# Turning masks over: TensorE transposes against transposing transfers, in a two-layer graph attention kernel

## The chip, the cores and the metric

The kernel runs on one core of a Trainium2 chip. A core has five engines with instruction queues of their own: PE (TensorE: matmuls and transposes, into PSUM), DVE (VectorE), ACT (ScalarE), POOL (GpSimd), and SP (SyncE, which here only issues transfers); 16 DMA engines move the data. The metric is the time of one execution on the device in microseconds (us), from the first instruction to the last.

## The reference

The input is x, 32 graphs (batches) of 512 nodes with 512 features, and for each graph an adjacency matrix of 512x512 integers. Two layers follow one another, each with a layer norm and a relu ahead of it and a residual sum behind it. Cut to what matters, for one graph:

```python
# layer 0: softmax over the row (axis -1), one head
h = maximum(layernorm(x), 0)
s = leaky_relu((h @ w_src)[:, None] + (h @ w_dst)[None, :] + b, 0.2)
x = x + softmax(where(adj + eye == 0, -inf, s), axis=-1) @ h

# layer 1: two GAT layers, softmax over the column (axis 0 of source x destination)
h = maximum(layernorm(x), 0)
mask = (adj > 0) | eye
def gat(h, W, a_src, a_dst):            # for each head
    xl = h @ W
    e = leaky_relu((xl @ a_src)[:, None] + (xl @ a_dst)[None, :], 0.2)
    return softmax(where(mask, e, -1e9), axis=0).T @ xl
h = elu(gat(h, W1, ...) + b1)           # 4 heads of 256, side by side
x = x + gat(h, W2, ...) + b2            # 1 head of 512
```

## The kernel before

Each 512x512 matrix of a batch is held as four row tiles of 128 partitions, `[P, T, N]` with P = 128, T = 4, N = 512. A mask is such a matrix in bf16 that holds 0 where there is an edge and a very large negative number (`NO_EDGE`) where there is none, so that masking is an addition.

**Two orientations of each mask.** The softmax weights E are computed with the source on the partitions, in the layout that the following matmul takes as its stationary operand, and the maximum that the softmax subtracts is taken along the free dimension of the opposite layout. So `edge_weights` (L473) wants a mask twice: `mask_max` for the maximum, `mask` for the weights. Layer 0 gives it `m0` and `m0T`; the five calls of layer 1 (four heads, then the second GAT layer, which the code calls layer 2) give it `m1T` and `m1`. T stands for the transpose.

`edge_weights` runs, for one head:

- `spread` (L462): four PE transposes that put a column of scores into every partition of one PSUM place, `m_row` (one place) or `c_row` (one place);
- `largest` (L480, DVE), four times: the maximum over `mask_max` plus that row;
- two small DVE operations (L486, L488) that make of it the value m to subtract, a second `spread` of m into `m_row` and one of the other scores into `c_row`;
- for each of four tiles: leaky relu on ACT (L498), minus m on DVE (L501), plus `mask` on POOL (L503), exponential on ACT (L506).

Then `aggregate` (L509) multiplies E with the values on PE (L516), into the PSUM places `acc` (four of them).

**How the masks are made.** `masks0` (L566) and `masks1` (L588) load the adjacency of a batch, as bf16, through POOL's queue (L552), turn it into the mask on DVE (L572, L577, L580 for m0; L593, L599 for m1), and call `transposed_mask` (L555). That makes 16 PE transposes of 128x128 bf16 blocks (recorded at L417, in `pe_transpose`) with an identity in bf16 (`ident_b`), four into each of four `acc` places, and four copies out of PSUM by ACT (L450) or DVE (L456), whichever the plan finds free (`evict`, L446).

**Order.** The kernel is written as a list of operations, which `Plan` (L35) orders before anything is emitted. Each operation has an engine (or two to choose from), a cost that is a pair (ns that it keeps its engine or queue, ns until its result is there), and the buffers that it reads and writes. The plan walks through time: on the engine that is free first it starts the ready operation that stands earliest in the list; an operation with `ahead` counts as so many places earlier (`AHEAD` is 400). A buffer gets one of a fixed number of places (`slots`, L243) when an operation on it starts, and gives it back after its last one. `m0`, `m0T`, `m1`, `m1T` and `adj` have one place each, `E` three, `x` two. The SP queue and the issue of transfers are planned as engines too. What comes out is a fixed order of instructions on each engine; at run time each waits on semaphores for what it really needs.

The main loop (L866) works on several batches at once: in pass b it makes the mask of layer 1 and the projection for batch b (`masks1`, `layer1_project`), finishes batch b-1 (`layer2_out`), runs the four heads of batch b, and between them layer 0 of batch b+1 (`layer0_out`, `layer1_in`) and the scores of layer 0 of batch b+2. Batch x goes out to DRAM (`spill`) and comes back in between, on the SP queue, with the loads of x and the stores of the output. The projections (`products`, L665) use seven products of half-size blocks in place of eight, their matmuls are at L717.

Of the kernel before, what the change touches and what calls it, by code (L numbers as in the profile page):

```python
# [9 lines left out]
F32 = mybir.dt.float32  # L10
BF16 = mybir.dt.bfloat16
# [4 lines left out]
P = 128  # L16
# [18 lines left out]
class Plan:  # L35
# [11 lines left out]
    def op(self, engines, cost, emit, reads=(), writes=(), ahead=0, lock=None):  # L47


        i = len(self.ops)  # L50
        after = set()
        for buf, part in reads:
            after.update(buf.wrote.get(part, ()))
        for buf, part in writes:
            after.update(buf.wrote.get(part, ()))
            after.update(buf.read.get(part, ()))
        bufs = []
        for buf, part in (*reads, *writes):
            if buf.kind is not None and buf not in bufs:
                bufs.append(buf)  # L60
                buf.left += 1
                if buf.left == 1 and buf.kind in self.turns:
                    self.turns[buf.kind].append(buf)
        for buf, part in reads:
            buf.read.setdefault(part, []).append(i)
        for buf, part in writes:
            buf.wrote[part] = [i]
            buf.read[part] = []
        after.discard(i)
        self.ops.append((engines if isinstance(engines, tuple) else (engines,), cost, emit, after, bufs, i - ahead, lock))  # L70
# [89 lines left out]
                    known(j)  # L160


def on_pe(n, dtype=F32, transpose=False):
    if transpose:
        return (110.0, 300.0) if dtype == F32 else (68.0, 220.0)
    one = 2 * max(0.8376 * n + 2, 110.0)
    return one, one + 170.0


def on_dve(n, speed=1.0, scaled_psum=False):  # L170
    one = n / 0.96 / speed + (130.0 if scaled_psum else 70.0)
    return one, one + 85.0


def on_act(n, per_partition=0):

    one = n / 1.2 + (80.0, 140.0, 280.0)[per_partition]
    return one, one + 60.0


def on_pool(n, narrow=False):
    one = 2.04 * n + 70.0 if narrow else 2.2 * n + 100.0
    return one, one + 30.0
# [3 lines left out]
def kernel(  # L187
# [24 lines left out]
    nc = tc.nc  # L212
    B, N, D = x.shape
    H, F = att_src1.shape
    HF = H * F
    T = N // P
# [8 lines left out]
    const = ctx.enter_context(tc.tile_pool(name="const", bufs=1))  # L225
# [9 lines left out]
    def node_block(t: int) -> slice:  # L235
        return slice(t * P, (t + 1) * P)


    def places(kind, n, shape, dtype=F32, pool=big):
        return [pool.tile(shape, dtype, tag=f"{kind}{k}", name=f"{kind}{k}") for k in range(n)]  # L240
# [4 lines left out]
        "adj": places("adj", 1, [P, T, N], BF16),  # L245
        "m0": places("m0", 1, [P, T, N], BF16),
        "m0T": places("m0T", 1, [P, T, N], BF16),
        "m1": places("m1", 1, [P, T, N], BF16),
        "m1T": places("m1T", 1, [P, T, N], BF16),
        "h": places("h", 1, [P, T, D + 1]),  # L250
        "hT": places("hT", 1, [P, KD, N]),
# [19 lines left out]
    op = plan.op  # L271


    ident = const.tile([P, P], F32, name="ident")
    make_identity(nc, ident)
    ident_b = const.tile([P, P], BF16, name="ident_b")
    nc.vector.tensor_copy(ident_b, ident)
    off_diag = const.tile([P, P], BF16, name="off_diag")
    nc.vector.tensor_scalar(off_diag, ident, 0.0, None, op0=ALU.is_equal)
    minus_half = const.tile([P, T], F32, name="minus_half")  # L280
# [131 lines left out]
    ROW = range(T)  # L412

    def pe_transpose(ahead, dst, dst_of, src, src_of, identity, part):

        dtype = BF16 if identity is ident_b else F32
        op("PE", on_pe(P, dtype, True), lambda: nc.tensor.transpose(dst_of(), src_of(), identity), src, dst(part), ahead)  # L417

    def layernorm(X):

# [25 lines left out]
    def evict(src, dst, src_of, dst_of, n, bias=None, psum_half=False):  # L446

        def by_act():
            if bias is None:
                nc.scalar.copy(dst_of(), src_of())  # L450
            else:
                nc.scalar.activation(dst_of(), src_of(), AF.Identity, bias=bias)  # L452

        def by_dve():
            if bias is None:
                nc.vector.tensor_copy(dst_of(), src_of())  # L456
            else:
                nc.vector.tensor_scalar(dst_of(), src_of(), -1.0, None, op0=ALU.add)

        op(("ACT", "DVE"), (on_act(n, bias is not None), on_dve(n)), (by_act, by_dve), src, dst)  # L460
# [10 lines left out]
    AHEAD = 400  # L471

    def edge_weights(kind, scores, a_of, c_of, mask_max, mask, junk_of=None):  # L473

        a_row = spread("m_row", scores + mask_max(*ROW), a_of, AHEAD)
        amax, z, m = Buffer("col"), Buffer("col"), Buffer("col")
        for t in range(T):
            def largest(t=t):
                count[0] += 1
                nc.vector.tensor_tensor_reduce(  # L480
                    junk[count[0] % 2], mask_max.at[:, t, :], a_row.at, 1.0, LOWEST, ALU.add, ALU.max,
                    accum_out=amax.at[:, t : t + 1],
                )
            op("DVE", on_dve(N), largest, a_row(*ROW) + mask_max(t), amax(t))
        c_all = lambda: c_of(None)
        op("DVE", on_dve(T), lambda: nc.vector.tensor_add(z.at, c_all(), amax.at), scores + amax(*ROW), z(0))  # L486
        op(
            "DVE", on_dve(T), lambda: nc.vector.scalar_tensor_tensor(m.at, z.at, SLOPE, z.at, op0=ALU.mult, op1=ALU.max),  # L488
            z(0), m(0),
        )  # L490

        E = Buffer(kind)
        m_row = spread("m_row", m(0) + E("place"), lambda t: m.at[:, t : t + 1], AHEAD)
        c_row = spread("c_row", scores + E("place"), c_of, AHEAD)
        for t in range(T):
            op(
                "ACT", on_act(N, 1),
                lambda t=t: nc.scalar.activation(E.at[:, t, :], c_row.at, AF.Prelu, bias=a_of(t), scale=1.0, alpha=SLOPE),  # L498
                c_row(*ROW) + scores, E(t),
            )  # L500
            op("DVE", on_dve(N), lambda t=t: nc.vector.tensor_sub(E.at[:, t, :], E.at[:, t, :], m_row.at), m_row(*ROW) + E(t), E(t))  # L501
            op(
                "POOL", on_pool(N, True), lambda t=t: nc.gpsimd.tensor_add(E.at[:, t, :], E.at[:, t, :], mask.at[:, t, :]),  # L503
                E(t) + mask(t), E(t), lock=True,
            )
            op("ACT", on_act(N), lambda t=t: nc.scalar.activation(E.at[:, t, :], E.at[:, t, :], AF.Exp), E(t), E(t))  # L506
        return E
# [44 lines left out]
        op("POOL", (2200.0, 8000.0), lambda: nc.gpsimd.dma_start(a.at, node_tiles(adj, b)), (), a(0))  # L552
        return a

    def transposed_mask(m, mT, ahead):  # L555
        for k in range(T):
            pt = Buffer("acc")
            view = lambda pt=pt: pt.at[:, : N // 2].bitcast(BF16)
            for t in range(T):
                pe_transpose(  # L560
                    ahead, pt, lambda t=t, view=view: view()[:, node_block(t)], m(t) + mT("place"),
                    lambda t=t, k=k: m.at[:, t, node_block(k)], ident_b, t,
                )
            evict(pt(*ROW), mT(k), view, lambda k=k: mT.at[:, k, :], N)

    def masks0(b):  # L566


        a, m0, m0T, d = load_adj(b), Buffer("m0"), Buffer("m0T"), Buffer("d")
        op(  # L570
            "DVE", on_dve(T * N, 4.0),
            lambda: nc.vector.tensor_scalar(m0.at, a.at, 0.0, NO_EDGE, op0=ALU.is_equal, op1=ALU.mult),  # L572
            a(0), m0(*ROW), lock=True,
        )
        for t in range(T):
            own = node_block(t)
            op("DVE", on_dve(P), lambda t=t, own=own: nc.vector.tensor_add(d.at[:, t, :], a.at[:, t, own], ident), a(0), d(t), lock=True)  # L577
            op(
                "DVE", on_dve(P),
                lambda t=t, own=own: nc.vector.tensor_scalar(  # L580
                    m0.at[:, t, own], d.at[:, t, :], 0.0, NO_EDGE, op0=ALU.is_equal, op1=ALU.mult
                ),
                d(t), m0(t), lock=True,
            )
        transposed_mask(m0, m0T, AHEAD)
        return m0, m0T

    def masks1(b):  # L588

        a, m1, m1T = load_adj(b), Buffer("m1"), Buffer("m1T")  # L590
        op(
            "DVE", on_dve(T * N, 4.0),
            lambda: nc.vector.tensor_scalar(m1.at, a.at, 0.0, NO_EDGE, op0=ALU.is_le, op1=ALU.mult),  # L593
            a(0), m1(*ROW), lock=True,
        )
        for t in range(T):
            own = node_block(t)
            op(
                "DVE", on_dve(P), lambda t=t, own=own: nc.vector.tensor_mul(m1.at[:, t, own], m1.at[:, t, own], off_diag),  # L599
                m1(t), m1(t), lock=True,  # L600
            )
        transposed_mask(m1, m1T, AHEAD)
        M[b] = (m1, m1T)

    slots["d"] = places("d", 1, [P, T, P], BF16)
# [311 lines left out]
```

## Time and profile before

| | |
|---|---|
| time, median of 3 runs | 3947.46 us (3946.25 to 3949.8) |
| span of the profiled run | 3948.1 us |
| two batches (from 1110.81 to 1350.72 us) | 239.91 us |
| PE busy in the first 119 us | 51.0 us |
| transposes of masks on PE (L417, bf16) | 1024, 220 ns each |
| copies of m0T and m1T out of PSUM | 132 on ACT (70.3 us), 124 on DVE (49.6 us) |
| transfers through SP and ACT queues | 138.42 MB + 2.88 MB |
| adjacency through POOL's queue | 33.56 MB |
| x load, spill, load back, output (1 MB each), issue to landing | 5.1, 4.3, 5.7, 4.3 us |
| adjacency load (0.5 MB), issue to landing | 5.8 us |

A row of the groups reads: line, engine, operation, output <- input with the tile names, shape, how many; then busy time and the mean length in ns of one; then how long the engine had been idle just before them and what ended that. In the order of time each row begins with its start and its length in us, and x4 says that four of the same kind in a row are merged. PE records two instructions for each f32 matmul of the program. A list of waits reads: who waited <- for whom: us in total, how many times, the longest. Time that an engine is idle matters only if something else had to wait for it.

### The profile page before, as it was taken

The numbers are of one execution on the slowest core, as the hardware profiler recorded it, in microseconds if no ns is written. First come the engines' busy times: TensorE is split into PE (matmuls) and PEld (weight loads), VectorE is DVE, ScalarE is ACT, GpSimd is POOL, SyncE is SP. The second block draws the span as 40 slices with busy tenths as digits, with TensorE's granted clock in tenths as the row PEclk, the third lists the DMA queues.
The fourth block names the chain that finished last, engine by engine and source line by source line (L and its number), as shares of the span: only waits on it lengthen the run. The fifth ranks groups of instructions, "written<-read, shape, count | busy, mean of one in ns | idle before, by whom it ended". The sixth has DMA issues, their size and how long they took to land.

```text
span 3948.1 us, 54741 instructions
## 1 busy us (share of the span) xinstructions
PE 3860.7 (98%) x20224; PEld 3342.0 (85%) x20224; DVE 2926.7 (74%) x7733; ACT 1715.3 (43%) x2991; POOL 1478.0 (37%) x1306
## 2 busy tenths in 40 slices
PE   4899999999999999999999999999999999999998
PEld 3788888888888888888888888888888888888887
DVE  6887767777777777777777677777777777777764
ACT  2444444444444454444444444444444544444432
POOL 3434333344333343343343433443343433433421
PEclk8999999999999999999999999999999999999999
DMA  4011111111111111111111111111111111111100
GB/s 136 6 54 54 33 49 49 33 54 52 30 49 54 33 54 33 49 49 33 54 54 33 47 50 33 54 44 37 49 48 39 54 33 49 49 33 54 49 22 22
DMA packets 107421, 178.36 MB, mean 45 GB/s; under 512 B 3728, under 2 KB 40592, under 8 KB 107152
## 3 DMA queue, kind: packets, MB, share of 16 engines
q1 hardware_dynamic: 72064, 138.42, 9.5%
q0 software_dynamic: 33792, 33.56, 5.4%
q8 instruction: 158, 2.59, 0.3%
q10 hardware_dynamic: 1296, 2.88, 0.2%
q14 instruction: 111, 0.91, 0.1%
HBM read 141.30 MB, written 67.11 MB: 53 GB/s over the span
## 4 chain that ended last, share of the span: by engine, by line
PE 96%; DVE 2%; DMA 1%; POOL 1%; issue 1%; ACT 0%; SPq 0%; DVEq 0%; ACTq 0%; POOLq 0%
PE acc L516 45%; PE sums L717 22%; PE acc L717 17%; PE acc L417 6%; PE m_row L417 4%; PE c_row L417 2%; DVE junk L307 1%; POOL E_one L503 1%; DMA w<-in_L_gnn_W_dram 0%; DVE E_one L501 0%; ACT E_one L506 0%; DVE junk L480 0%; DMA x<-in_x_dram 0%; DMA w_T<-in_L_gnn_W_dram 0%; DVE w_T L399 0%
## 5 line engine op out<-in xcount | busy, mean ns | idle before, releaser
L516 PE MATMUL acc<-pair,E 128*128 128x257 f32 x4096 | 913.2, 380 | 0.0
L503 POOL TENSOR_TENSOR E<-E,m 128x512 f32<-128x512 f32 x512 | 577.6, 1157 | 825.3 <-DVE E L501 818.3
L516 PEld LDWEIGHTS acc<-pair,E 128*128 128x128 f32 x4096 | 769.2, 189 | 119.2 <-ACT pair L452 5.5
L516 PE MATMUL acc<-h,E_one 128*128 128x256 f32 (+1 forms) x2048 | 501.6, 384 | 6.3 <-ACT E_one L506 3.9
L791 ACT ACTIVATE e<-v,minus_one 128x512 f32<-128x512 f32 x256 | 184.7, 722 | 717.8 <-DVE v L782 682.4
L516 PE MATMUL acc<-xl,E_one 128*128 128x257 f32 (+1 forms) x2048 | 479.5, 381 | 2.7 <-ACT E_one L506 2.7
L480 DVE CUSTOM_DVE_ANT_0 junk<-m1T,m_row 128x512 bf16<-128x512 bf16 x640 | 411.1, 682 | 51.5 <-PE m_row L417 50.9
L506 ACT ACTIVATE E<-E 128x512 f32<-128x512 f32 x512 | 323.6, 632 | 229.6 <-POOL E L503 227.8
L516 PEld LDWEIGHTS acc<-xl,E_one 128*128 128x128 f32 x2048 | 378.6, 190 | 51.8 <-ACT E_one L506 3.1
L516 PEld LDWEIGHTS acc<-h,E_one 128*128 128x128 f32 x2048 | 367.1, 191 | 55.6 <-ACT E_one L506 13.8
L501 DVE TENSOR_TENSOR E<-E,m_row 128x512 f32<-128x512 f32 x512 | 330.3, 679 | 14.7 <-PE m_row L417 12.2
L498 ACT ACTIVATE E<-c_row,pair 128x512 f32<-128x512 f32 x512 | 314.6, 690 | 48.6 <-PE c_row L417 47.7
L717 PE MATMUL acc<-w_T,E 128*128 128x257 f32 (+1 forms) x1024 | 268.1, 384 | 14.7 <-DVE x L534 14.7
L794 DVE SCALAR_TENSOR_TENSOR v<-e,v 128x512 f32<-128x512 f32 x256 | 177.7, 694 | 138.8 <-ACT e L791 134.6
L534 DVE SCALAR_TENSOR_TENSOR x<-acc,r,x 128x256 f32<-128x256 f32 x512 | 244.8, 479 | 46.3 <-PE acc L516 43.7
L717 PE MATMUL sums<-w_T,E 128*128 128x257 f32 (+1 forms) x1024 | 271.6, 381 | 0.0
L717 PE MATMUL acc<-w,E 128*128 128x257 f32 (+1 forms) x1024 | 264.6, 381 | 0.0
L503 POOL TENSOR_TENSOR E_one<-E_one,m0T 128x512 f32<-128x512 f32 x128 | 146.5, 1176 | 309.8 <-DVE E_one L501 309.8
L506 ACT ACTIVATE E_one<-E_one 128x512 f32<-128x512 f32 x256 | 161.3, 630 | 232.1 <-POOL E_one L503 228.9
L782 DVE SCALAR_TENSOR_TENSOR v<-acc,r,b_r 128x256 f32<-128x256 f32 x512 | 246.2, 481 | 13.7 <-DVE r L779 0.4
L779 DVE RECIPROCAL r<-acc 128x1 f32<-128x1 f32 x512 | 83.5, 163 | 214.1 <-PE acc L516 211.5
L503 POOL TENSOR_TENSOR E_one<-E_one,m 128x512 f32<-128x512 f32 x128 | 144.3, 1160 | 234.1 <-DVE E_one L501 234.1
(123 smaller groups left out, 6750.1 us busy)
## 6 DMA issues: line engine op xcount, KB each, us to landing
x<-in_x_dram SPq DMA_DIRECT2D x32, 1024.0 KB, 5.1
adj<-in_adj_dram POOLq DMA_DIRECT2D x64, 512.0 KB, 5.8
spill<-x SPq DMA_DIRECT2D x32, 1024.0 KB, 4.3
x<-spill SPq DMA_DIRECT2D x32, 1024.0 KB, 5.7
out_dram<-x SPq DMA_DIRECT2D x32, 1024.0 KB, 4.3
w<-in_L_gnn_W_dram SPq DMA_DIRECT2D x6, 256.0 KB, 9.0
w<-in_L_gnn_W_dram SPq DMA_DIRECT2D x8, 127.5 KB, 4.9
w_T<-in_L_gnn_W_dram SPq DMA_DIRECT2D x4, 128.5 KB, 5.8
```

The costliest lines, as they stand in the source:

```text
L417: op("PE", on_pe(P, dtype, True), lambda: nc.tensor.transpose(dst_of(), src_of(), identity), src, dst(part), ahead)
L480: nc.vector.tensor_tensor_reduce(junk[count[0] % 2], mask_max.at[:, t, :], a_row.at, 1.0, LOWEST, ALU.add, ALU.max, accum_out=amax.at[:, t ...
L498: lambda t=t: nc.scalar.activation(E.at[:, t, :], c_row.at, AF.Prelu, bias=a_of(t), scale=1.0, alpha=SLOPE),
L501: op("DVE", on_dve(N), lambda t=t: nc.vector.tensor_sub(E.at[:, t, :], E.at[:, t, :], m_row.at), m_row(*ROW) + E(t), E(t))
L503: "POOL", on_pool(N, True), lambda t=t: nc.gpsimd.tensor_add(E.at[:, t, :], E.at[:, t, :], mask.at[:, t, :]),
L506: op("ACT", on_act(N), lambda t=t: nc.scalar.activation(E.at[:, t, :], E.at[:, t, :], AF.Exp), E(t), E(t))
L516: lambda s=s: nc.tensor.matmul(acc.at[:, :n], E.at[:, s, node_block(t)], of(s), start=(s == 0), stop=(s == T - 1)),
L534: lambda acc=acc, r=r, f=f, t=t: nc.vector.scalar_tensor_tensor(X.at[:, t, f], acc.at[:, :HD], r.at, X.at[:, t, f], op0=ALU.mult, op1=ALU. ...
L717: lambda k=k: nc.tensor.matmul(acc.at[:, :width], at[a]()[:, k, node_block(r)], weight_of(w, k, c), start=(first and k == 0), stop=(k == n ...
L782: lambda t=t, acc=acc, r=r: nc.vector.scalar_tensor_tensor(v.at[:, t, :], acc.at[:, :F], r.at, b1_r[:, h * F : (h + 1) * F], op0=ALU.mult, ...
L791: op("ACT", on_act(2 * F, 1), lambda e=e, ts=ts: nc.scalar.activation(e.at, v.at[:, ts, :], AF.Exp, bias=minus_one), parts, e(0))
L794: lambda e=e, ts=ts: nc.vector.scalar_tensor_tensor(v.at[:, ts, :], e.at, 1.0, v.at[:, ts, :], op0=ALU.min, op1=ALU.max),
```

## The change

The masks are no longer turned over by PE and copied out of PSUM. Each mask is turned over by four transfers from SBUF to SBUF, one for each row tile, that transpose on the way; each takes a 128x512 tile of bf16 (128 KB) and fills a column block of the transposed mask. All are issued on the SP queue, and the plan is told that each keeps the queue for 2300 ns and lands after 6000 ns, so that it sets them one behind the other. PE, ACT and DVE lose the work, and `acc` is no longer used for masks.

Since a transfer fills a piece of every row tile of the transposed mask, readers now depend on all four (`mask_max(*ROW)`, `mask(*ROW)`). And `m1` gets a second place, so that the mask of the next batch may be written while the one before is still read; `m1T` keeps one. The bf16 identity goes. Nothing of what is computed changes.

```diff
-        "m1": places("m1", 1, [P, T, N], BF16),
+        "m1": places("m1", 2, [P, T, N], BF16),
...
-    ident_b = const.tile([P, P], BF16, name="ident_b")
-    nc.vector.tensor_copy(ident_b, ident)
...
-            op("DVE", on_dve(N), largest, a_row(*ROW) + mask_max(t), amax(t))
+            op("DVE", on_dve(N), largest, a_row(*ROW) + mask_max(*ROW), amax(t))
...
-                E(t) + mask(t), E(t), lock=True,
+                E(t) + mask(*ROW), E(t), lock=True,
...
-    def transposed_mask(m, mT, ahead):
-        for k in range(T):
-            pt = Buffer("acc")
-            view = lambda pt=pt: pt.at[:, : N // 2].bitcast(BF16)
-            for t in range(T):
-                pe_transpose(
-                    ahead, pt, lambda t=t, view=view: view()[:, node_block(t)], m(t) + mT("place"),
-                    lambda t=t, k=k: m.at[:, t, node_block(k)], ident_b, t,
-                )
-            evict(pt(*ROW), mT(k), view, lambda k=k: mT.at[:, k, :], N)
+    def transposed_mask(m, mT):
+        for t in range(T):
+            op(
+                "SP", (2300.0, 6000.0),
+                lambda t=t: nc.sync.dma_start(mT.at[:, :, node_block(t)], m.at[:, t, :], transpose=True),
+                m(t), mT(t),
+            )
...
-        transposed_mask(m0, m0T, AHEAD)
+        transposed_mask(m0, m0T)
...
-        transposed_mask(m1, m1T, AHEAD)
+        transposed_mask(m1, m1T)
```

More of the change, by code (lines that the diff above doesn't have):

```diff
@@ L160, in run, with on_pe @@
                     known(j)
-def on_pe(n, dtype=F32, transpose=False):
+def on_pe(n, transpose=False):
     if transpose:
-        return (110.0, 300.0) if dtype == F32 else (68.0, 220.0)
+        return 110.0, 300.0
     one = 2 * max(0.8376 * n + 2, 110.0)
@@ L414, in pe_transpose @@
     def pe_transpose(ahead, dst, dst_of, src, src_of, identity, part):
-        dtype = BF16 if identity is ident_b else F32
-        op("PE", on_pe(P, dtype, True), lambda: nc.tensor.transpose(dst_of(), src_of(), identity), src, dst(part), ahead)
+        op("PE", on_pe(P, transpose=True), lambda: nc.tensor.transpose(dst_of(), src_of(), identity), src, dst(part), ahead)
     def layernorm(X):
```

## The prediction, written before the changed kernel was run

> **What bounds the kernel now.** I read the page from the top: busy shares first, then the slices.
>
> ```profile
> PE 3860.7 (98%) x20224; PEld 3342.0 (85%) x20224; DVE 2926.7 (74%) x7733; ACT 1715.3 (43%) x2991; POOL 1478.0 (37%) x1306
> ...
> PE   4899999999999999999999999999999999999998
> PEld 3788888888888888888888888888888888888887
> DVE  6887767777777777777777677777777777777764
> ```
>
> A busy share may hide waits inside pipelined matmuls, so I asked for two things more: the waits of PE between 119 and 3700 us, and the busy time of each engine over one repeat of the pattern, which takes two batches because x and spill have two places.
>
> ```profile
> PE acc L717 <- DVE x L534: 14.7, 1, 14.7
> PE acc L516 <- ACT pair L452: 0.2, 1, 0.2
> ```
>
> ```profile
> core 0: us, PE busy (x) PEld busy (x) DVE busy (x) ACT busy (x) POOL busy (x), PEclk, DMA share, GB/s
> ...
> 1110.81:1350.72 239.91, 239.77 (x1265) 208.04 (x1265) 180.39 (x476) 106.81 (x187) 91.46 (x82) 1.00 0.15 45
> ```
>
> In 3581 us PE waits 14.9 us, and 14.7 of that is one wait at the very beginning, the last of the start-up. One repeat lasts 239.91 us and PE is busy for 239.77 of it at full clock; DVE has a quarter free, the DMA engines 85%. So from 119 us to the end the kernel runs at the speed of PE: an instruction that leaves PE is paid back in full, and one that leaves DVE or ACT is paid back only if it held PE up. The first 119 us are another stage (PE waits 16.4 us for the first mask and 14.2 us for a maximum; DVE is busy 88.7 of 119 us).
>
> What is to leave PE are the bf16 transposes of the masks:
>
> ```profile
> L417 PE MATMUL acc<-ident_b,m 128*128 128x128 bf16 x1024 | 78.0, 220 | 19.1 <-DVE m L580 18.0 <-DVE x L534 0.7 <-ACT m1T L450 0.3
> L450 ACT COPY m0T<-acc 128x512 bf16<-128x512 bf16 x67 | 35.4, 579 | 9.2 <-PE acc L417 9.2
> L450 ACT COPY m1T<-acc 128x512 bf16<-128x512 bf16 x65 | 34.9, 589 | 37.2 <-PE acc L417 35.4
> L456 DVE COPY m1T<-acc 128x512 bf16<-128x512 bf16 x63 | 25.5, 423 | 28.0 <-PE acc L417 28.0
> L456 DVE COPY m0T<-acc 128x512 bf16<-128x512 bf16 x61 | 24.1, 417 | 14.8 <-PE acc L417 14.8
> ```
>
> 1024 x 220 ns would be 225 us, but 220 ns is how long one takes from end to end; they overlap. What one takes from PE is the distance between starts, and that is in the order of time:
>
> ```profile
> 1187.58 1.06 PE L417 MATMUL acc<-ident_b,m 128*128 128x128 bf16 x16
> 1188.47 0.60 PE L417 MATMUL c_row<-ident,pair 128*128 128x128 f32 x4
> ...
> 1218.13 1.12 PE L417 MATMUL acc<-ident_b,m 128*128 128x128 bf16 x16
> 1219.20 7.20 PE L516 MATMUL acc<-pair,E 128*128 128x257 f32 x32
> ```
>
> Sixteen (m1) push the next instruction back by 0.89 us, sixteen (m0) by 1.07 us.
>
> [...]
>
> **The change, part by part.** *PE.* I added, from the order of time, the distance from the start of each run of mask transposes to the next instruction. After 119 us that is 57.3 us (980 records, 58 ns each, 1.8 to 2.0 us a batch). The earlier ones (13.4 us with the waits between them) lie where PE is idle anyway: worth nothing. So PE gives back 57.3 us.
>
> *The 256 copies out of PSUM*, 70.3 us of ACT and 49.6 us of DVE, go too. Neither engine held PE up, so nothing is added for them. The same for the identity cast.
>
> *256 transfers of 128x512 bf16 (128 KB)* are added, 8 a batch, on the SP queue with x, spill and output. Bytes are no matter: 1 MB a batch beside some 5.5 MB at a DMA share of 0.15. What matters is who waits. In the built program, the `largest` op of layer 1's first head (DVE, L480 before) waits for all four transfers into m1T; m0T is filled almost a whole batch ahead of the Pool addition that reads it, and has time. And since m1 has two places, m1 of batch b+1 is written one batch early; its transfers do not wait for the mask but for m1T's place, that is for the last `largest` of layer 2. SP's order is: two m0T transfers (they wait for the last Pool addition that reads the old m0T), four m1T, two m0T, output, x, spill, load back.
>
> The room that this leaves, on the clock of the repeat above, from the orders of time of Pool, DVE and PE (start, length):
>
> ```profile
> 1171.01 4.51 POOL L503 TENSOR_TENSOR E_one<-E_one,m0T 128x512 f32<-128x512 f32 x4 [9.61 <-DVE E_one L501]
> ...
> 1178.29 0.68 DVE L480 CUSTOM_DVE_ANT_0 junk<-m1T,m_row 128x512 bf16<-128x512 bf16 x1
> ...
> 1171.28 1.03 PE L717 MATMUL sums<-w,hT 128*128 128x258 f32 x4
> ```
>
> m0T is free at 1175.5, or 1176.3 with the 0.8 us of an adjacency issue that now stands ahead on Pool; m1T is free at about 1178.9. The need: in the new order the m_row transposes of head 0 stand behind 41 of the 56 projection matmuls of hT (before: 32), 0.435 us each, plus 3.5 us of others, so at 1171.3 + 17.8 + 3.5 = 1192.6. With s the spacing of transfers on the queue and l the time from issue to landing, the last m1T lands at about 1176.3 + 5s + l (if s is above 1.3): in time if 5s + l is at most 16.3 us.
>
> The trace bounds s and l from below: a plain load of 128.5 KB lands 3.1 us after issue and SP issues in 0.36 us, so 5s + l is about 5. [...] Between lie the planner's own 2300 and 6000 ns: 17.5, at the edge. I take the middle with room, at most 2.3 and about 4: for every other transfer the planner's time to landing can be compared, and it is near or above what is measured (x 5.5 to 5.1, spill 5.0 to 4.3, load back 5.5 to 5.7, adjacency 8.0 to 5.8). Then nothing waits. Cost 0.
>
> What a late transfer would hold: DVE is in order, and the copies and additions that free acc, sums and m_row stand behind the `largest`. The next m_row transposes come 7 matmuls (3.0 us) later on PE and need m_row back, which the four `largest` (2.4 us) hold. So PE has about half a microsecond; beyond it, each microsecond late costs about one a batch, 31 us in all.
>
> *First 119 us.* The first m0T transfers stand on SP behind 24 weight loads and the second x load, issued at 29.3 us. Four at 2.3 and 4 land by 29.7 + 6.9 + 4 = 40.6; Pool's first addition starts at 42.6. Hidden[...]. Some copies leave DVE there, which is worth 1 to 3 us. I count 0, from -3 to +8.
>
> Sum: 3947.5 - 57.3 = **3890**.
>
> **The rivals.** *A, a wait at the edge:* 5s + l is about 17.5, the `largest` waits 1 us a batch: 3890 + 31 = 3921. For it: the planner's numbers give just that. Against: they were no underestimates elsewhere. *B, slow transfers, slower than before:* [...] *C, a hidden collision:* the adjacency load (issued at 1187.4, 5.8 us, lands at 1193.2) shares the DMA engines with m1T, and DVE's d additions (L577) now come right behind the `largest`, at about 1195. Four microseconds more make 2 us of wait a batch: 3890 + 62 = 3952, no change. Against: a DMA share of 0.15.
>
> **How the numbers follow.** Forecast 0.73; A 0.11; B 0.11; C 0.05. The predicted time is the forecast's, 3890. Low end 3870: 10 us at the start, if it ends earlier by more than the copies, and the 10.6 us of waits in the last 100 us, which another order may remove. High end 3955: it takes in A up to 2 us late and C, and leaves out B and a little more. Within 0.2% means 3939.6 to 3955.4: C, and a tail of A, 0.06; faster 0.80; slower 0.14 (B, and A beyond 2 us).
>
> **What would show it.** Right: no bf16 matmuls; a repeat of about 236.1 us instead of 239.9 with PE still busy throughout; the DVE `largest` on m1T waiting for PE's m_row, not DMA. Wrong: `largest` <- DMA m1T in the list of waits and PE m_row <- DVE behind it (A, B); d <- DMA adj (C); or a repeat shorter by less than 3.8 us with PE full, which would mean that a transpose takes less of PE than the distance between starts says.

## The result, and the profile after

| | before | after |
|---|---|---|
| time, median (lowest to highest), 4 runs each | 3948.39 us (3946.25 to 3949.8) | 3885.7 us (3883.76 to 3885.97) |
| span of the profiled run | 3948.1 us | 3882.0 us |
| period: one batch, mean of 20 batches in the middle | 119.956 us | 117.506 us |
| span less 31 periods (start and end) | 229.5 us | 239.3 us |

The ratio is 0.9841, with a 95% interval of 0.9824 to 0.9858: 62.7 us, or 1.6%, faster. (The two profiled executions are 66.1 us apart.) The period is the distance between the issues of the output on the SP queue. It and the rest part the difference in two: 31 x (119.956 - 117.506) = 76.0 us won in the steady part, 9.8 us lost at the two ends, together the 66.1.

The page of the changed kernel, busy shares and slices:

```profile
PE 3782.1 (97%) x19200; PEld 3282.0 (85%) x19200; DVE 2834.0 (73%) x7559; ACT 1647.6 (42%) x2890; POOL 1498.4 (39%) x1324
...
PE   3799999999999999999999999999999999999998
```

The 1024 bf16 transposes are gone (20224 to 19200 instructions) and PE is still busy in nearly every slice. One repeat of two batches, between two outputs, has the columns of the one shown for the kernel before:

```profile
1088.79:1323.79 235.00, 235.00 (x1201) 204.49 (x1200) 174.04 (x465) 102.64 (x181) 92.59 (x83) 1.00 0.21 54
```

235.0 us where it was 239.91, PE full at full clock, DVE still a quarter free, and the DMA share 0.21 in place of 0.15. The waits of PE from 119 to 3700 us are:

```profile
PE acc L414 <- DVE v L788: 4.2, 5, 2.6
PE acc L513 <- ACT pair L449: 1.2, 1, 1.2
PE acc L513 <- ACT hT L447: 0.5, 1, 0.5
PE acc L414 <- ACT h L437: 0.2, 1, 0.2
```

All of that lies ahead of 391 us; from there to 3390 no wait of PE is listed at all. In the order of time on SP, the eight transfers of a batch (start and length; x4 merges four) look like this:

```profile
1162.87 3.40 SPq L556 DMA_TRANSPOSE m0T<-m  x2
1166.66 5.24 SPq L556 DMA_TRANSPOSE m1T<-m  x4
1171.94 2.58 SPq L556 DMA_TRANSPOSE m0T<-m  x2
1206.28 0.38 SPq L833 DMA_DIRECT2D out_dram<-x  x1
```

The same for the whole run, gathered by tile for m1T, shows what a transfer costs (shortest, median and longest ns) and what their reader waits for:

```profile
L477 DVE CUSTOM_DVE_ANT_0 junk<-m1T,m_row x640: 670/682/690, 129.6 to 3855.1; 128x512 bf16<-128x512 bf16 x160
L556 SPq DMA_TRANSPOSE m1T<-m x128: 1188/1259/2182, 62.0 to 3754.4; - x128
its engine sat idle before it (us, times) until:
  PE m_row L414: 145.2, 124
...
DMA to landing us min/median/max: 2.4/2.5/6.2
```

The queue is held 1.26 us by a transfer, and the data are there 2.5 us after issue. The maximum that reads m1T never waits for DMA, only for PE's m_row. The place of each transfer in the batch follows from two rows, of Pool and of DVE:

```profile
1158.34 4.50 POOL L500 TENSOR_TENSOR E_one<-E_one,m0T 128x512 f32<-128x512 f32 x4 [0.55 <-DVE E_one L498]
```

```profile
1181.53 0.69 DVE L477 CUSTOM_DVE_ANT_0 junk<-m1T,m_row 128x512 bf16<-128x512 bf16 x1 [0.38 <-PE m_row L414]
```

Pool gives m0T back at 1162.84 and the first transfer is issued at 1162.87. The last m1T transfer is issued at about 1170.6 and is there at about 1173.1; the maximum that needs it begins at 1181.53, 8.4 us later. From the release of m0T to the maximum there are 18.7 us; the transfers use 10.3 of them, and 8.4 are left.

### The profile page after: what moved, and what is told of

It is laid out like the page before. It is cut to its first block, busy times and chain, and to the rows that moved or that the text cites. A ratio compares the mean times of both kernels' runs of the same rounds, so it can differ in the third digit from the quotient of the medians.

```text
span 3882.0 us, 52830 instructions
## 1 busy us (share of the span) xinstructions
PE 3782.1 (97%) x19200; PEld 3282.0 (85%) x19200; DVE 2834.0 (73%) x7559; ACT 1647.6 (42%) x2890; POOL 1498.4 (39%) x1324
## 2 busy tenths in 40 slices
DMA packets 246677, 211.82 MB, mean 55 GB/s; under 512 B 142992, under 2 KB 179856, under 8 KB 246416
## 3 DMA queue, kind: packets, MB, share of 16 engines
q1 hardware_dynamic: 211328, 172.01, 14.5%
## 4 chain that ended last, share of the span: by engine, by line
PE 95%; DVE 3%; DMA 1%; ACT 1%; issue 0%; POOL 0%; SPq 0%; ACTq 0%; DVEq 0%
PE acc L513 45%; PE sums L711 23%; PE acc L711 17%; PE m_row L414 4%; PE acc L414 4%; PE c_row L414 2%; DVE junk L305 1%; DMA w<-in_L_gnn_W_dram 1%; DVE v L788 0%; ACT e L785 0%; DVE v L776 0%; DVE junk L477 0%; DVE E L498 0%; DMA w_T<-in_L_gnn_W_dram 0%; DVE st L420 0%
## 5 line engine op out<-in xcount | busy, mean ns | idle before, releaser
L513 PE MATMUL acc<-h,E_one 128*128 128x256 f32 (+1 forms) x2048 | 489.4, 382 | 6.8 <-ACT E_one L503 5.5
L447 ACT COPY pair<-sums 128x258 f32<-128x258 f32 x293 | 110.0, 376 | 348.5 <-PE sums L711 346.6
L711 PEld LDWEIGHTS acc<-w_T,E 128*128 128x128 f32 x1024 | 193.9, 190 | 42.6 <-DVE x L531 14.2
```

Source lines behind the costliest of these rows:

```text
L513: lambda s=s: nc.tensor.matmul(acc.at[:, :n], E.at[:, s, node_block(t)], of(s), start=(s == 0), stop=(s == T - 1)),
L711: lambda k=k: nc.tensor.matmul(acc.at[:, :width], at[a]()[:, k, node_block(r)], weight_of(w, k, c), start=(first and k == 0), stop=(k == n ...
```

## The experiments

My theory after the result: in the steady part PE sets the time, what is won is PE's slots, and the transfers are hidden. But 2.45 us a batch are won where the prediction counted 1.8 to 2.0. Three candidates for the rest were the second place of m1, the copies out of acc, and a slowing of the matmuls that stand beside a bf16 transpose. In the table, the ratio is given by its 95% interval, and "rest" is the span less 31 periods.

| kernel | time, us | ratio to before, 95% interval | period | rest |
|---|---|---|---|---|
| m1 with two places, masks on PE | 3945.12 | 0.9983 to 0.9999 | 119.66 | 233.1 |
| changed, m1 with one place | 3922.84 | 0.9921 to 0.9946 | 118.68 | 240.5 |
| changed, PE transposes back | 3932.44 | 0.9945 to 0.9970 | 119.26 | 234.7 |
| the same, copies to one spare place | 4033.23 | 1.0198 to 1.0226 | 122.44 | 235.3 |
| the same, copies to spare tiles | 4029.24 | 1.0189 to 1.0217 | 122.42 | 233.9 |
| the same, in the old positions | 3954.58 | 1.0008 to 1.0021 | 119.95 | 234.3 |
| changed, transfers in 2 pieces | 3889.41 | 0.9831 to 0.9861 | 117.59 | 243.7 |
| changed, transfers in 4 pieces | 4202.91 | 1.0627 to 1.0656 | 128.23 | 226.7 |
| changed, measured costs in the plan | 3888.88 | 0.9834 to 0.9861 | 117.59 | 242.5 |
| only layer 0's mask on PE | 3921.18 | 0.9918 to 0.9942 | 118.99 | 230.1 |
| only layer 1's mask on PE | 3919.05 | 0.9911 to 0.9936 | 118.51 | 242.8 |
| changed, first masks on PE | 3880.76 | 0.9814 to 0.9840 | 117.53 | 235.6 |

### The second place of m1

Alone, on the kernel before:

```diff
-        "m1": places("m1", 1, [P, T, N], BF16),
+        "m1": places("m1", 2, [P, T, N], BF16),
```

> The kernel before, with the second place for layer 1's mask and nothing else; masks still turned over on PE. My theory: PE keeps all its 1024 transposes and was full already, so no change: 3948, within 6 us. Rival (part of the gain comes from the mask being written a batch early): 2.48 us a batch were saved where the slots of the transposes explain 1.87, so the second place alone would bring the other 0.6, about 19 us: 3929.

Measured: 3945.12 us, 0.30 us a batch less. That is inside the 6 us that the theory allowed, but it is not nothing: the interval of the ratio ends just below 1. And taken out of the changed kernel (the same line turned back):

> The changed kernel, with one place for layer 1's mask. The transfers into m1T can then start only once the mask of this batch is written, some 7 us later than in the changed kernel. My theory: the weights of the first head had about 10 us to spare before PE wants them, and the plan moves the row of scores later, so little is lost: 3886 to 3900. Rival (the second place is what hides the transfers): the maximum waits 5 us or more in each batch: 3886 + 31 x 5 = 4040.

Measured: 3922.84 us, between the two, so that both expectations missed. The place is worth 37 us beside the transfers and about 4 without them. From 391 to 3390 us, where the changed kernel has no listed wait of PE, this one has two:

```profile
PE acc L513 <- ACT pair L449: 11.2, 13, 0.9
PE m_row L414 <- DVE col L485: 9.2, 13, 0.7
```

20.4 us in 25 batches are 0.8 of the 1.17 us that a batch grew by. With one place the m1T transfers begin later, beside a load of adjacency on POOL's queue, and both become slower. In the order of time, then in the list of issues (median us to landing), then in the waits of DVE from 391 to 3390 us:

```profile
1182.67 5.28 SPq L556 DMA_TRANSPOSE m1T<-m  x4
```

```profile
1182.48 0.82 POOL L549 DMA_DIRECT2D adj<-in_adj_dram  x1 [1.21 <-DVE m L587]
```

```profile
adj<-in_adj_dram POOLq DMA_DIRECT2D x64, 512.0 KB, 6.6
m0T<-m SPq DMA_TRANSPOSE x128, 5.0
m1T<-m SPq DMA_TRANSPOSE x128, 5.8
```

```profile
DVE m L566 <- DMA adj<-in_adj_dram: 21.2, 16, 2.5
```

In the changed kernel the transfers land 2.5 us after issue and the adjacency after 5.7, and DVE waits for no transfer from 391 us on. That is the collision of the prediction's rival C, in this kernel. Whether it is what makes PE's two waits is not shown. The transfers without the second place win 26 us of the 63.

### The PE work put back, with nothing that uses it

To the changed kernel, beside the transfers (the bf16 identity, not shown, is back too):

```diff
+        for k in range(T):
+            pt = Buffer("acc")
+            view = lambda pt=pt: pt.at[:, : N // 2].bitcast(BF16)
+            for t in range(T):
+                op(
+                    "PE", (68.0, 220.0),
+                    lambda t=t, k=k, view=view: nc.tensor.transpose(view()[:, node_block(t)], m.at[:, t, node_block(k)], ident_b),
+                    m(t), pt(t), AHEAD,
+                )
```

> The changed kernel, and PE does its 1024 bf16 transposes too, into the same PSUM places; nobody copies or reads them (the masks used are those of the transfers). It prices the PE slots alone. My theory (slots of 58 ns, 1.87 us a batch; the other 0.6 us were short waits for the copies): 3886 + 57 = 3943, the mean distance of the other matmuls stays at 216.6 to 217.4 ns. Rival (a switch between bf16 and f32 on PE costs the neighbours time): 3886 + 31 x 2.48 = 3963, and that distance goes back to about 218.

Measured: 3932.44 us, 11 us below the theory's 3943, in part because the rest is 4.6 us shorter. The period grows by 1.75 us; the distances from start to start of these 32 transposes, added up over 24 batches, are 1.78 us a batch. That is the prediction's price for PE's slots, in a kernel that differs in nothing else but the order that the plan makes of it. The f32 matmuls other than transposes hold their distance (217.5 ns on average in 24 batches from 400 us on, 217.4 in the changed kernel), so the third candidate is out: no slowing beside a bf16 transpose is seen here.

### The copies

The same kernel, with the 256 copies out of acc by ACT or DVE, which nothing reads. First into one spare place that is handed out like other buffers:

```diff
+            jT = Buffer("jT")
+            evict(pt(*ROW), jT(0), view, lambda jT=jT: jT.at, N)
```

> As the one before, and the transposes are also copied out of PSUM, by ACT or DVE as the plan finds them free, into one spare place of SBUF that nobody reads. So all of the old work is back, beside the transfers. My theory: the copies cost another 0.6 us a batch by short waits: about 3943 + 18 = 3961, with the distance of the other matmuls at about 218. Rival (copies are free, the neighbours of bf16 transposes paid): the same time as the one before, within 6 us.

Measured: 4033.23 us, 101 us above the transposes alone; both expectations missed. I suspected the single spare place, in which the copies wait for one another, and gave each engine a tile of its own that is not handed out:

```diff
+            op(
+                ("ACT", "DVE"), (on_act(N), on_dve(N)),
+                (
+                    lambda view=view: nc.scalar.copy(junk_act, view()),
+                    lambda view=view: nc.vector.tensor_copy(junk[count[0] % 2], view()),
+                ),
+                pt(*ROW), (),
+            )
```

> The changed kernel with the 1024 bf16 transposes on PE and the 256 copies out of acc by ACT or DVE back, but the copies go to spare tiles that are not handed out (one of ACT's, one of DVE's), so that no copy waits for another engine's; nothing reads them. The transposes alone made 3932; two places alone, with both for real, 3945. If the copies, and the acc places that they hold, are what is left of the saving (theory), this is 3945 within 8. If the copies are free once no spare place is short (rival, which is how the prediction counted them), it is 3932 within 5. Above 3960 would mean that transfers and copies together disturb each other.

Measured: 4029.24 us, so it was not the spare place; and it is above the 3960 that would speak for transfers and copies disturbing each other. The waits of PE from 391 to 3390 us say what it is:

```profile
PE acc L516 <- ACT pair L452: 23.1, 25, 0.9
PE acc L417 <- DVE v L808: 14.1, 25, 0.6
PE acc L516 <- DVE x L534: 6.2, 24, 0.3
PE acc L516 <- ACT junk_act L574: 5.9, 25, 0.2
```

Four waits for an acc place, once a batch each: 2.0 of the 3.16 us by which a batch is longer than with the transposes alone. The list counts a wait only from the end of the instruction before it. Counted from start to start, these four and a fifth, too short to be listed, take 2.9 of the 3.16 us. And in the order of time the mask transposes stand elsewhere than before the change:

```profile
1368.11 0.83 PE L568 MATMUL acc<-ident_b,m 128*128 128x128 bf16 x12
1369.20 7.20 PE L516 MATMUL acc<-pair,E 128*128 128x257 f32 x32 [0.26 <-DVE x L534]
...
1377.55 0.61 PE L568 MATMUL acc<-ident_b,m 128*128 128x128 bf16 x8
1378.72 0.66 PE L417 MATMUL acc<-ident,v 128*128 128x128 f32 x4 [0.57 <-DVE v L808]
1380.31 7.21 PE L516 MATMUL acc<-pair,E 128*128 128x257 f32 x32 [0.92 <-ACT pair L452]
```

They are strewn among the transposes of v and the aggregations, which need acc places at once. In the kernel before, they also held the place of the transposed mask, and so began only when that was free. One word puts this back:

```diff
-                    m(t), pt(t), AHEAD,
+                    m(t) + mT("place"), pt(t), AHEAD,
```

> As the kernel with the PE transposes and the copies to spare tiles (4029), but the transposes now also hold the place of the transposed mask, as they did in the kernel before; this brings them back, in the built order, to where they stood there: sixteen in a row ahead of an aggregation, and six and ten among the projections, instead of four and the other 28 strewn among aggregations and transposes of v. Work and transfers are the same. If the price of the copies depends on where the plan puts them, by the acc places that they hold (theory), this is close to the kernel with two places for layer 1's mask and all masks on PE (3945): 3937 to 3953, and the 2 us a batch of waits of PE for acc are gone. If transfers and copies disturb each other by running together (rival), it stays at about 4029 and above 4000.

Measured: 3954.58 us. That is 1.6 us above the interval that I gave, but 75 us below the 4029 of the same work in other positions. Of the waits one is left:

```profile
PE acc L568 <- ACT junk_act L574: 9.3, 25, 0.4
```

So transfers beside copies do not disturb each other much, and the price of the copies is for the most part the acc places that they hold, at the moment at which they hold them. In the old positions it is 119.95 - 119.26 = 0.69 us a batch against the transposes alone; the kernel with two places and real masks on PE, which has no transfers, is 0.40 above the same. The copies (in the second comparison, with the readers' waiting for real masks) therefore cost 0.4 to 0.7 us a batch, not nothing. In the first comparison 0.37 of the 0.69 are in the list of waits, 0.54 from start to start. In the second nothing is listed, but 0.17 of the 0.40 are longer distances among the mask transposes: once a batch an aggregation behind them waits 0.10 us more for ACT's copy of m0T, and one of them 0.07 us more for DVE. For the other 0.23 no cause is shown.

### How much room the transfers have

Each transfer issued as two of 128x256, then as four of 128x128, in the same order of work. The edit for four:

```diff
-                lambda t=t: nc.sync.dma_start(mT.at[:, :, node_block(t)], m.at[:, t, :], transpose=True),
+                lambda t=t: [
+                    nc.sync.dma_start(mT.at[:, k, node_block(t)], m.at[:, t, node_block(k)], transpose=True) for k in range(T)
+                ],
```

> The changed kernel with each transposing transfer issued as two of half the columns (128x256), one behind the other; the order of the work is unchanged. Measured in the changed kernel: 1.25 us of queue for one transfer of 128 KB, 2.5 us to landing. If the queue is held by the instruction (theory), an issue stays at about 1.25 us, a tile takes s = 2.5 us, and 5s + l = 12.5 + 2.5 = 15 us is still within the 16.3 us of the prediction: 3886, at most 3900. If it is held by the bytes or blocks (rival), an issue takes about 0.65 us, s stays 1.25, and the time is 3886 as well. The length of an issue tells them apart, the time does not.

> The changed kernel with each transposing transfer issued as four, one for each 128x128 block; order unchanged. If the queue is held by the instruction (theory), a tile takes s = 5.0 us, 5s + l = 27.5 us, which is 11.2 us beyond the room of 16.3 that the prediction worked out; less its half microsecond, at about 1 us a batch for each: 31 x 10.7 = 330, so about 4215, with the DVE maximum of layer 1 waiting about 10 us a batch for the transfers into m1T, and PE m_row waiting for DVE behind it. If it is held by the bytes or blocks (rival), an issue takes about 0.35 us, s stays 1.25, and the time is that of the changed kernel, 3886 within 8. A time between the two with issues of 1.25 us would mean that the room is larger than the prediction had it.

Measured: 3889.41 and 4202.91 us. A tile in two pieces takes twice, in four pieces four times as long on the queue. The m1T transfers with two pieces, with four, and with four again in the order of time:

```profile
L557 SPq DMA_TRANSPOSE m1T<-m x256: 1168/1244/2406, 65.6 to 3763.8; - x128
```

```profile
L557 SPq DMA_TRANSPOSE m1T<-m x512: 1093/1230/2401, 74.6 to 4083.7; - x171
```

```profile
1117.23 10.03 SPq L557 DMA_TRANSPOSE m0T<-m  x8
1127.36 21.02 SPq L557 DMA_TRANSPOSE m1T<-m  x16
```

An instruction of 128, 64 or 32 KB into m1T holds the queue for 1.26, 1.24 and 1.23 us. With four pieces a tile takes s = 21.02 / 4 = 5.26 us and 5s + l is 28.7; that is over the room, and the chain that the prediction described appears, in the waits of PE and of DVE from 391 to 3390 us (23 batches):

```profile
PE m_row L414 <- DVE col L477: 190.3, 23, 8.9
```

```profile
DVE junk L477 <- DMA m1T<-m: 189.1, 70, 7.7
```

The maximum waits 8.2 us a batch for m1T, and PE behind it 8.3 us for m_row. The loss is 128.23 - 117.51 = 10.7 us a batch, the number that was expected, but not all of it is waiting. After the wait PE runs more slowly for some us (it does so after all three waits of 8.2 to 8.3 us between 3580 and 3850 us), as in the order of time and, for the first of the three, in the granted clock (the last but two of the columns, 0.50):

```profile
3587.58 1.11 PE L414 MATMUL m_row<-ident,pair 128*128 128x128 f32 x4 [8.23 <-DVE col L477]
3588.48 1.93 PE L713 MATMUL sums<-w_T,E 128*128 128x258 f32 x4
3590.20 1.93 PE L713 MATMUL acc<-w,E 128*128 128x258 f32 x4
3591.92 1.57 PE L713 MATMUL sums<-w_T,hT 128*128 128x258 f32 x4
3593.33 1.03 PE L513 MATMUL acc<-xl,E_one 128*128 128x257 f32 x4
```

```profile
3587.60:3592.80 5.20, 5.20 (x15) 4.27 (x16) 3.48 (x14) 0.37 (x1) 0.00 (x0) 0.50 0.13 25
```

Four records of matmuls take 1.93 us there, and 1.03 before the wait and again from 3593.33 on. In 24 batches from 400 us on, such stretches cost 2.3 us a batch beyond the usual distances, and the waits, from start to start, 8.4: together the 10.7. The agreement with the expected number is therefore luck. The sum 5s + l is rough for pieces as well: the last piece of the last tile is issued 3.9 us after the first, but the first transfer goes out at 1117.23, before m0T is wholly free, since its first piece needs only the first of Pool's four additions:

```profile
1116.05 4.51 POOL L500 TENSOR_TENSOR E_one<-E_one,m0T 128x512 f32<-128x512 f32 x4 [0.54 <-DVE E_one L498]
```

With two pieces 5s + l is about 15, or 16 to the last piece, and a loss is not seen beyond 4 us.

### The costs in the plan

```diff
-                "SP", (2300.0, 6000.0),
+                "SP", (1300.0, 2600.0),
```

> The changed kernel with the plan told what the transfers really take (1300 ns of queue, 2600 ns to landing, where it was told 2300 and 6000). Theory: no transfer is waited for in the steady part, so nothing can be won there; at the start the plan may order the first batches otherwise: 3886, from 3875 to 3892. Rival: the pessimistic costs made the plan put transfers or their readers late, at about 0.5 us a batch: about 3870 or less, with a shorter repeat than 235.0 us for two batches.

Measured: 3888.88 us with the period 0.08 us longer, as the theory had it. The plan's too high costs cost nothing.

### One mask at a time

Layer 0's mask on PE with its copies, layer 1's by transfers with two places; then the reverse. The line of the first that differs from the kernel before (the function that issues the transfers and the second place of m1 come with it):

```diff
-        transposed_mask(m1, m1T, AHEAD)
+        transferred_mask(m1, m1T)
```

> Half of the change: layer 1's mask is turned over by transfers and has two places, layer 0's mask is still turned over by PE and copied out of acc by ACT or DVE. The prediction's slots for m0 are the dearer half (1.07 us for sixteen against 0.89), so if a batch pays for its slots alone and the rest of the saving (some 0.6 us a batch) goes with the copies half and half (theory), PE's part is 31 x (1.07 + 0.3) = 42 us of the 63, less the 14 us at the start which the filler on PE gives back in part: 3910 to 3925. Rival: the unlisted part of the saving is all due to layer 1's mask (its place and the wait for it), then only the slots stay: 3886 + 33 - 5 = about 3910 or below.

> The other half: layer 0's mask by transfers, layer 1's mask by PE and copies, with its two places. With both halves back the time is 3945 (two places alone), with none 3886, and with layer 0's mask back 3921, which is 35 us above the changed kernel. If the halves add up (theory), this one loses the other 24 of the 59 us: 3910. Its slots are 1024/2 x 58 ns, less those at the start: 27 to 30 us. Rival: the halves do not add up, since a mask on PE takes acc places and copies that trouble the other as well; then both halves lose more than half of 59 and this one is at 3920 or above.

Measured: 3921.18 us, within what the theory gave, and 3919.05 us, which is 9 above the theory and just under the rival's bound. The two lose 35.5 and 33.4 us against the changed kernel, together 68.9, while both at once lose 59.4 (3945.12). In the periods it is 1.49 and 1.00 us a batch, together 2.49, and 2.15 for both at once. So the halves add up only roughly: the second mask to go to PE costs somewhat less than the first, and no trouble of one through the other, as the rival had it, is seen. In the first of the two, PE waits once a batch for ACT's copy of m0T:

```profile
PE acc L417 <- ACT m0T L450: 9.4, 25, 0.4
```

### The start

The rest (start and end) is 229.5 us before and 239.3 after. PE was idle for 76.2 of the first 119 us in the changed kernel, and for 68.0 before. The first output shows what the start loses; before, changed, and changed with the edit below:

```profile
259.21 0.38 SPq L839 DMA_DIRECT2D out_dram<-x  x1
```

```profile
266.18 0.39 SPq L833 DMA_DIRECT2D out_dram<-x  x1
```

```profile
261.40 0.38 SPq L853 DMA_DIRECT2D out_dram<-x  x1
```

It goes out 7.0 us later in the changed kernel; the other 2.8 of the 9.8 us come after it. So I turned over the first masks as before:

```diff
+        if b < 2:
+            transposed_mask(m0, m0T, AHEAD)
+        else:
+            transferred_mask(m0, m0T)
```

with the same for m1 and b < 1.

> The changed kernel, but the first two masks of layer 0 and the first of layer 1 are turned over by PE and copied out, since PE was idle for 76 us of the first 119 in the changed kernel. If the 14 us of idle time that the start gained are due to the missing work on PE's side and to transfers behind the weight loads (theory), up to 8 of them come back: 3878 to 3884. If the start is bound by DVE, which is busy 38.8 of the 39 us from 80 to 119 (rival), the copies cost as much as they save: 3884 to 3892.

Measured: 3880.76 us (3880.21 to 3882.05), ratio 0.9827 to before. The first output is 4.8 us earlier than in the changed kernel, and the rest 3.7 us shorter. It is the fastest version of the study: its runs lie wholly below those of the changed kernel (3883.76 to 3885.97). The two were measured beside runs of the kernel before that agree within 0.6 us, but not side by side.

## Why the prediction was right, and where its terms were off

*PE bounds from 119 us on, and the mask's slots come back in full: right.* The repeat is 235.0 us with PE full, no bf16 matmul is left, and the transposes alone, put back, cost 1.75 us a batch for 1.78 us of slots. Over 31 batches that is 54 us, against 57.3 in the prediction. The distances from start to start (58 ns a transpose by the prediction's count) gave the right size; 1024 times the 220 ns from end to end would have been 225 us.

*Copies, and m1's second place, worth nothing: wrong in size.* The steady part won 76.0 us where 57.3 were counted. "Neither engine held PE up" was read from a list of waits that has almost none. But there is time that the list does not show. In 24 batches from 400 us on, the distances between starts sum, for the 480 records of a batch's f32 matmuls other than transposes, to 104.96 us in the kernel before, 104.51 with the second place of m1 alone, and 104.36 in the changed kernel; the mask transposes take 1.87 us of a batch in the kernel before. So 1.87 of the 2.45 us are slots and 0.60 is time that the matmuls lost. The runs part the 2.45 another way: 0.30 us for the second place of m1 alone, 0.40 from there to the transposes alone beside the transfers (the copies, and the masks being really read from PE's results), and 1.75 from there to the changed kernel. These three are steps of one chain of kernels, so that they must add up; in another order the shares are different, since the second place is worth 1.17 us a batch once the transfers are there. That the copies cost short waits for acc is shown where these become long (the copies in other positions), and for 0.17 of the 0.40 us; for the rest it is only argued.

*The first 119 us counted at 0, from -3 to +8: the start lies inside that range, the end does not appear in the sum.* The 8 was the author's estimate and was not shown by a trace. Start and end together cost 9.8 us; 7.0 of them are lost by the first output. PE is idle 8.2 us more in the first 119, and 5.8 us more from there to 391, but a part of that is only the work that it no longer has. With the first masks on PE 3.7 us of the two ends come back. The rest I did not trace; the plan makes another order of the first batches in each kernel, and the rest of all versions that run without late transfers lies between 229.5 and 243.7 us. The two misses have opposite signs: the steady part won 18.7 us more than counted, and the ends lost 9.8. That is why the sum is closer (3885.7 against 3890) than its terms are; this closeness is luck.

*Transfers in time if 5s + l is at most 16.3 us: right that they are in time, and the sum of the right form.* s is 1.25 and l 2.5, so 5s + l is 8.8 (10.3 in the batch shown, where the first two transfers took 3.40 us); the prediction had taken up to 2.3 and 4, an estimate from the plan's numbers, and its lower bound was 5. The room in the changed kernel, from m0T's release (1162.84) to the maximum (1181.53), is 18.7 us and not 16.3. At about 15 us next to nothing is lost (0.08 us a batch); at 28.7 us the time is 4203, with the chain DMA, DVE, PE as described. Between the two the edge itself is not tested. That each microsecond late costs about one was too little where PE waits for long: 8.4 us of waiting cost 10.7.

*Rival A (wait at the edge)* falls since s and l, 1.25 and 2.5 us, are far under the plan's 2.3 and 6. *Rival B (slow transfers)* falls for the changed kernel, where s is 1.25 us; how slow the transfers might be was not shown by any trace before the result. Its mechanism was right. In the run with four pieces s is 5.26 us and l 2.4 us, and the time is 317 us above that of the changed kernel: PE waits 8.3 us a batch, and another 2.3 us a batch are lost in the slower stretches behind the waits (granted clock 0.50 in the one shown). There a block of 128x128 takes 1.31 us of the queue (21.02 us for sixteen) and lands after 2.4; what keeps the changed kernel fast is that four blocks in one instruction take hardly longer than one (medians of 1.26 and 1.23 us into m1T). *Rival C (adjacency)* is not seen in the changed kernel: from 391 to 3390 us PE has no listed wait, and DVE none for DMA. There the transfers of the batch shown (the first issued at 1162.87, the last at about 1173.3) lie between its two adjacency loads (issued at 1156.97 and 1174.59, landed at 1162.5 and 1180.4). With one place for m1 they lie beside one, and the collision is there.

## What to carry to other kernels

Where one engine is full, price an instruction that leaves it by the distance between starts (here 1.78 us a batch, for 1.75 that it cost), and copies that empty its PSUM places at more than nothing even if no wait is listed: the same 256 copies cost from 0.4 to 3.2 us a batch, by the position that the plan gave them. For work moved to a DMA queue, write the room from the release of its place to its first reader in terms of spacing and landing; one run with the spacing stretched then tests the room itself. Look for a buffer that the moved work needs earlier, since its second place belongs to the change: here it is worth about 4 us alone and 37 us with the transfers. And do not price a long wait of PE by its length alone: in the run with four pieces 8.4 us of waiting a batch were followed by 2.3 us lost to slower matmuls (granted clock 0.50 in the stretch shown).

## What was not expected of the hardware

- A transposing transfer from SBUF to SBUF keeps the SP queue for 1.22 to 1.26 us (medians), whether it carries 32, 64 or 128 KB, while a plain transfer of 1 MB keeps it for 0.36 to 0.38. At these sizes it is priced by the instruction. The measured pace on the queue is that of the issues, 128 KB in 1.25 us or 105 GB/s.
- At the median it lands 2.4 to 2.5 us after issue at all three sizes, though a transfer of 128 KB is recorded as 544 packets (211328 packets on the queue, 72064 before, for 256 transfers), and the packets under 512 bytes grow by as many (from 3728 to 142992 in all). In the kernel with one place for m1, where the transfers run beside the adjacency load, it is 5.0 and 5.8 us.
- In the run with four pieces PE's granted clock is 0.50 from 3587.60 to 3592.80, right behind a wait of 8.23 us, as shown above.
